# Local transformer as listed operations per engine, with the norms spread by transfers

## The chip, the cores and the metric

The kernel runs on one core of a Trainium2 chip. The metric is the device time of one execution in microseconds (us); smaller is better. A core has five engines that run their own instruction streams: TensorE (PE, matrix products, results into the PSUM memory), VectorE (DVE), ScalarE (ACT), GpSimd (POOL) and SyncE (SP, which here only issues transfers). Sixteen DMA engines move the data. Engines wait for one another through semaphores, and each works off its own instructions in the order in which they were written down.

## The reference

The program is a stack of twelve small blocks on 8 sequences of 256 tokens with 128 features. Two of its blocks are the same six-layer local transformer, and the change is in these. A layer is an attention over windows of 32 tokens that look back one window, and a gated feed-forward block. In the attention:

```python
qkv = x @ Wqkv                      # 128 -> 3 * 1024, 16 heads of 64
q = l2norm(q) * qs                  # t / max(norm(t), 1e-12)
k = l2norm(k) * ksc
q = q * cos * scale + rotate_half(q) * sin * scale
k = k * cos * inv + rotate_half(k) * sin * inv
sim = jnp.einsum('bhwie,bhwje->bhwij', bq, bk2) * QK_SCALE   # 32 rows, 64 keys
sim = jnp.where(mask, -jnp.finfo(sim.dtype).max, sim)
attn = jax.nn.softmax(sim, -1)
out = jnp.einsum('bhwij,bhwje->bhwie', attn, bv2)
return out.transpose(0, 2, 1, 3).reshape(b, n, INNER) @ Wo
```

The feed-forward block is a layer norm, a product to 2 x 341 features, `a * gelu(gate)`, and a product back to 128. Ahead of both, half of the features are shifted by one token. All numbers are 32-bit floats.

## The kernel before, in words

Activations lie features by tokens: a tile has 128 partitions (features) and T = 512 columns, two sequences of 256 tokens. There are four such groups (`NG`), and a layer treats them one after the other. A pair of layer and group is a unit. Inside a unit the sixteen heads are taken four at a time; such a *quad* is the step that the text counts in. A stage of six layers has 6 x 4 x 4 = 96 quads, and the program has two such stages.

`ffn2` is a software pipeline, written out by hand: in one pass of its loop `q0`, `q1`, `q2`, `q3` are four consecutive quads at different stages, and the calls in the loop set the order of every engine's instructions (`_Ordered` pins it). What happens to a quad:

- `quad_project` multiplies the unit's input `l_xs` by the weights of keys, then queries, into the PSUM tile `pp`. ACT squares it (`l_sq`). DVE multiplies it by the cosine table (`l_yk`, `l_yq`) and swaps neighbouring partitions (`l_yr`); POOL multiplies `l_yr` by the sine table and adds the two.
- `quad_norms` sums the squares by head on PE into `bank`; `quad_roots` turns them into inverse roots `l_rn` on ACT (a logarithm, an exponential), and SP moves four rows at a time, in four transfers, into the tile `l_rt`. In the next pass `quad_pick` spreads them over the partitions with four DVE shuffles, and `quad_keys` multiplies keys (`l_kp`) and queries (`l_yq`) by them on POOL.
- `quad_scores` forms the scores `sc`, masks included, on PE; DVE takes the maximum and subtracts it (`l_mx`, `l_e`); ACT exponentiates.
- `quad_turn` transposes the exponentials on PE (`et`) and ACT copies them (`l_at`).
- `quad_values` forms the values `vp`; ACT copies them to `l_v`, with a 65th column of ones for each head, and two SP transfers make a copy `l_w` that is shifted by one window.
- `quad_weigh` multiplies weights and values into `cx`, with the weights as the stationary operand (64x32) and the values moving (65 columns); the last column is the softmax's sum, by which DVE divides. `quad_back` transposes the result on PE (`ct`), and `quad_done` copies it (`l_ct`).

After the fourth quad, `local_rest` does the output product (`wo_acc`), the residual, the layer norm and the gated feed-forward in pieces between the quads of the next unit.

PSUM has three two-bank tiles (`two`: `pp`, `sc`, `vp`, `et`, `cx`, `ct`, `ge` take turns), one bank for sums and one for accumulators. In the profile most of these instructions carry line 285, the line of `_Ordered`'s helper, so that they are told apart by their tiles.

Of the kernel before, what the change touches and what calls it, by code (L numbers as in the profile page):

```python
# [28 lines left out]
P = 128  # L29
B, S, D = 8, 256, 128  # L30
NB = 2
# [21 lines left out]
def _constants():  # L53
# [59 lines left out]
    c["ksin"] = two(np.sin(fr) * (f(1.0) / sc) * sgn)  # L113
# [180 lines left out]
class _Net:  # L294
# [952 lines left out]
    def local_rows(self):  # L1247

        gp = self.nc.gpsimd
        one = lambda n, i, shape: self.work(f"{n}{i}", shape, bufs=1)  # L1250

        self.xs = [one("l_xs", i, (P, T)) for i in range(4)]
        for t in self.xs:
            gp.memset(t[64:, 0::S], 0.0)
        self.n_pad = 0

        self.rt = one("l_rt", 0, (P, T))
        gp.memset(self.rt, 0.0)
        self.low_masks(("lrow", "lmask"))

    def window_rows(self):

        gp = self.nc.gpsimd
        one = lambda n, i, shape: self.work(f"{n}{i}", shape, bufs=1)

        self.kp = [one("l_kp", i, (P, 2 * NB, WIN + S)) for i in range(1)]
        for t in self.kp:
            gp.memset(t[:, :, :WIN], 0.0)

        self.vs = [[one(n, i, (P, 4, 4, 65)) for n in ("l_v", "l_w")] for i in range(2)]  # L1270
        for v, w in self.vs:
            gp.memset(w, 0.0)
            for t in (v, w):
                gp.memset(t[:, :, :, 64:], 1.0)
# [12 lines left out]
    def local_tables(self, i):  # L1287

        out = {}
        for k in ("kcos", "ksin", "qcos", "qsin"):  # L1290
            t = self.work("l_" + k, (P, S), bufs=2)
            scale = self.get(f"F{i}_{k[0]}_scale" + ("_p" if k[1:] == "sin" else ""))
# [4 lines left out]
    def quad_project(self, q, n):  # L1297

        nc = self.nc
        four = lambda a: a.rearrange("p j (b s) -> p (j b) s", b=NB)  # L1300
        o = S if n == "k" else 0
        pp = self.two("pp")
        for j in range(2):
            self.mm(pp[:, j, :], q.w[:, o + P * j : o + P * (j + 1)], q.xs)
        sq = self.work("l_sq", (P, 2, T), bufs=4)
        nc.scalar.activation(sq, pp, AF.Square)
        y = self.work("l_y" + n, (P, 2, T), bufs=2)
        nc.vector.tensor_tensor(four(y), four(pp), q.tab[n + "cos"], ALU.mult)
        yr = self.work("l_yr", (P, 2, T), bufs=2)
        nc.vector.stream_shuffle(yr, pp, [i ^ 1 for i in range(32)])  # L1310
        nc.gpsimd.tensor_tensor(four(yr), four(yr), q.tab[n + "sin"], ALU.mult)
        nc.gpsimd.tensor_tensor(y, y, yr, ALU.add)
        q.y[n], q.sq[n] = y, sq

    def quad_values(self, q):
        nc = self.nc
        vp = self.two("vp").rearrange("p a b -> p (a b)")
        for m in range(4):
            self.mm(vp[:, S * m : S * (m + 1)], q.xs[:, P * m : P * (m + 1)], q.w[:, 2 * S :])
        v, w = self.vs[q.n % 2]  # L1320
        nc.scalar.copy(v.rearrange("p m h d -> p (m h) d")[:, :, :64],
                       vp.rearrange("p (n d) -> p n d", d=64))
        nc.sync.dma_start(w[32:], v[:96])
        nc.sync.dma_start(w[:32, 1::2], v[96:, 0::2])
        q.v = (w, v)

    def quad_norms(self, q):  # L1330
        sp = self.ps()
        for s, (n, j) in enumerate((("k", 0), ("q", 0), ("k", 1), ("q", 1))):
            self.mm(sp[32 * s : 32 * s + 32, :], self.get("hsum"), q.sq[n][:, j, :])
        q.sums = self.work("l_rn", bufs=1)
        self.nc.vector.tensor_scalar(q.sums, sp, 1e-24, None, ALU.max)

    def quad_roots(self, q):
        nc = self.nc
        rn = q.sums
        self.act(rn, rn, AF.Ln, scale=2.0**SH)  # L1340
        self.act(rn, rn, AF.Exp, bias=self.get("eps", 3, 1), scale=-0.5)
        for s in range(4):
            nc.sync.dma_start(self.rt[s::32], rn[32 * s : 32 * s + 32 : 8, :])

    def quad_pick(self, q):
        nc = self.nc
        q.r = {}
        for n, o in (("k", 0), ("q", 1)):
            r = q.r[n] = self.work("l_sq", (P, 2, T), bufs=4)
            for j in range(2):  # L1350
                nc.vector.stream_shuffle(r[:, j, :], self.rt, [2 * j + o] * 32)

    def quad_keys(self, q):

        nc = self.nc
        q.kp = self.kp[q.n % len(self.kp)]
        seq = lambda a: a.rearrange("p j (b s) -> p (j b) s", b=NB)
        nc.gpsimd.tensor_tensor(q.kp[:, :, WIN:], seq(q.r["k"]), seq(q.y["k"]), ALU.mult)
        nc.gpsimd.tensor_tensor(q.y["q"], q.y["q"], q.r["q"], ALU.mult)

    def quad_scores(self, q):

        nc = self.nc
        sc = self.two("sc")
# [19 lines left out]
        sl = lambda a: a.rearrange("p (n k) -> p n k", k=64)  # L1384
        bc = lambda a: a.unsqueeze(2).to_broadcast([P, 16, 64])
        sv = sl(sc.rearrange("p h n -> p (h n)"))
        mx = self.work("l_mx", (P, 16), bufs=2)
        nc.vector.tensor_reduce(mx, sv, AX.X, ALU.max)
        e = self.work("l_e", (P, 2 * T), bufs=2)
        nc.vector.tensor_tensor(sl(e), sv, bc(mx), ALU.subtract)  # L1390
        q.e = e

    def quad_exp(self, q):
        self.act(q.e, q.e, AF.Exp)

    def quad_turn(self, q):

        nc = self.nc
        tp = self.two("et").rearrange("p a b -> p (a b)")
        for n in range(8):  # L1400
            nc.tensor.transpose(tp[:, P * n : P * (n + 1)], q.e[:, P * n : P * (n + 1)],
                                self.get("ident"))
        q.at = self.work("l_at", (P, 2 * T), bufs=1)
        nc.scalar.copy(q.at, tp)

    def quad_weigh(self, q):

        nc = self.nc
        q.cx = []
        for j in range(2):  # L1410
            cp = self.two("cx")[:, :, : 4 * 65].rearrange("p x (n d) -> p x n d", d=65)
            for b in range(NB):
                for h in range(2):
                    for jj in range(4):
                        for x in range(2):
                            ks = slice(64 * x, 64 * x + 64)
                            o = P * (4 * h + 2 * j + b) + 32 * jj
                            self.mm(cp[32 * jj : 32 * jj + 32, x, 2 * b + h, :],
                                    q.at[ks, o : o + 32],
                                    q.v[jj % 2][ks, 2 * b + jj // 2, 2 * j + h, :])  # L1420
            rc = self.work("l_rc", (P, 2, 4), bufs=2)
            nc.vector.reciprocal(rc, cp[:, :, :, 64])
            cx = self.work("l_cx", (P, 2, 4, 64), bufs=4)
            nc.vector.tensor_tensor(cx, cp[:, :, :, :64],
                                    rc.unsqueeze(3).to_broadcast([P, 2, 4, 64]), ALU.mult)
            q.cx.append(cx)

    def quad_back(self, q):

        nc = self.nc  # L1430
        tp = q.tp = self.two("ct")
        for j in range(2):
            to = tp[:, j, :].rearrange("p (b c x i) -> p b x c i", b=NB, c=2, x=2)
            for b in range(NB):
                for x in range(2):
                    nc.tensor.transpose(
                        to[:, b, x], q.cx[j][:, x, 2 * b : 2 * b + 2].rearrange("p h d -> p (h d)"),
                        self.get("ident"))

    def quad_done(self, q):  # L1440
        ct = self.work("l_ct", (P, 2, T), bufs=5)
        self.nc.scalar.copy(ct, q.tp)
        q.unit.ct.append(ct)

    def local_rest(self, u):


        nc, i = self.nc, u.i
        acc = self.bank1("wo_acc")

        def project(cs):
            for c in cs:
                self.mm(acc, u.w["wo"][:, c, :], u.ct[c // 2][:, c % 2, :], start=c == 0, stop=c == 7)

        project(range(3))
        yield False
        project(range(3, 6))
        yield False
        yield False
        project(range(6, 8))  # L1460
        u.x1 = self.new_x()
        nc.vector.tensor_tensor(u.x1, acc, self.ys[u.g], ALU.add)
        if i == DEPTH - 1 and u.g == NG - 1:
            self.rest = u
            return
        xs = self.shifted(u.x1)
        yield False

        yield False
        self.settle()  # L1470
        xc, r = self.scratch("ln_c"), self.scratch("ln_r")
        m = self.bank1("mean")
        self.mm(m, self.get("mean"), xs)
        nc.vector.tensor_tensor(xc, xs, m, ALU.subtract)
        sq = self.scratch("ln_sq")
        nc.scalar.activation(sq, xc, AF.Square)
        yield True
        yield True
        v = self.bank1("var")
        self.mm(v, self.get("mean"), sq)  # L1480
# [9 lines left out]
        for f in u.early:  # L1490
            f()
# [330 lines left out]
```

## Time and profile before

| | |
|---|---|
| three runs | 5218.33, 5218.47, 5227.95 us; median 5218.47 |
| profiled execution | span 5219.8 us (from the first to the last instruction; no other time of it is listed) |
| granted TensorE clock, mean | 0.973 |
| first local stage | its first product starts at 955.6 us, its last quad's at 2611.8 |
| second local stage | 2921.4 to 4556.2 |
| PE, DVE, ACT, POOL busy | 94%, 69%, 48%, 58% of the span |
| DMA | 151.76 MB, 61390 packets |

How to read it: an engine's share is an average over the whole program; the table by stretches, shown further down, says what it is inside one stage. A group of instructions has its line, engine and operation, the tiles it writes and reads, the shape and the count, then its busy time in us and the mean ns of one, then the idle time before it and what ended that.

### The profile page before, as it was taken

What the parts mean: (1) busy time and instruction counts of PE and PEld (TensorE: products, weight loads), DVE (VectorE), ACT (ScalarE), POOL (GpSimd) and SP (SyncE); (2) the same over time, 40 slices, a digit from 0 to 9 for tenths busy, and PEclk for the clock granted to TensorE, in tenths of its full rate; (3) what the DMA queues carried; (4) which work ended last, traced back from release to release, by engine and by line L of the source; (5) the groups of instructions that cost most, each with busy time, mean ns of one, the idle gap of its engine ahead of it and who ended that gap; (6) DMA issues with size and microseconds to landing.
All of it is one profiled execution on the core that took longest, in us unless ns stands there. A gap on an engine that the chain in (4) does not pass through costs nothing.

```text
span 5219.8 us, 156276 instructions
## 1 busy us (share of the span) xinstructions
PE 4887.5 (94%) x70032; PEld 2895.3 (55%) x70032; DVE 3599.4 (69%) x6390; ACT 2483.9 (48%) x3011; POOL 3033.2 (58%) x1543
## 2 busy tenths in 40 slices
PE   9999998899999999999988899999999999989889
PEld 6755764455555555555544455555555555555456
DVE  4445446777777877787745777877787778755655
ACT  2233225555555555555544455555555555543652
POOL 0011003688888887888720588888888888701520
PEclk9999998999999999999989999999999999999999
DMA  2000000111111111111000011111111111100000
GB/s 75 1 1 1 1 1 1 40 29 49 34 49 35 43 38 45 38 42 41 26 28 5 21 36 42 37 46 37 42 41 42 41 39 41 29 36 1 1 1 9
DMA packets 61390, 151.76 MB, mean 29 GB/s; under 512 B 11185, under 2 KB 25394, under 8 KB 60466
## 3 DMA queue, kind: packets, MB, share of 16 engines
q1 hardware_dynamic: 60722, 141.77, 8.9%
q8 instruction: 551, 9.03, 0.7%
q14 instruction: 117, 0.96, 0.1%
HBM read 44.93 MB, written 1.05 MB: 9 GB/s over the span
## 4 chain that ended last, share of the span: by engine, by line
PE 71%; DVE 14%; ACT 8%; issue 2%; POOL 1%; DMA 1%; SPq 1%; DVEq 0%; ACTq 0%; POOLq 0%
PE mm L340 11%; PE pp L285 8%; PE e_o L340 7%; PE wo_acc L285 7%; PE bank L285 6%; PE sc L285 5%; PE vp L285 5%; PE ge L285 5%; PE cx L285 3%; PE ct L285 3%; DVE l_sq L285 3%; PE w_acc L285 2%; DVE l_yr L285 2%; PE ms L285 2%; ACT l_ct L285 2%
## 5 line engine op out<-in xcount | busy, mean ns | idle before, releaser
L285 PE MATMUL pp<-l_xs,wqkv 128*128 128x512 f32 x1536 | 693.4, 594 | 5.5 <-DMA wqkv<-in_f_wqkv 3.8
L285 POOL TENSOR_TENSOR l_kp<-l_sq,l_yk 128x1024 f32<-128x1024 f32 x192 | 456.6, 2378 | 357.4 <-DVE l_sq L285 354.2
L285 ACT COPY l_v<-vp 128x1024 f32<-128x1024 f32 x192 | 194.6, 1014 | 693.5 <-PE vp L285 693.5
L285 DVE STREAM_SHUFFLE l_sq<-l_rt 128x512 f32<-128x512 f32 x768 | 515.7, 747 | 0.1
L285 DVE STREAM_SHUFFLE l_yr<-pp 128x1024 f32<-128x1024 f32 x384 | 510.2, 1329 | 0.0
L285 PEld LDWEIGHTS pp<-l_xs,wqkv 128*128 128x128 f32 x1536 | 292.6, 191 | 356.6 <-issue 327.2
L340 PE MATMUL mm<-x,m 128*128 128x512 f32 x1024 | 479.4, 608 | 0.0
L285 POOL TENSOR_TENSOR l_yq<-l_yq,l_sq 128x1024 f32<-128x1024 f32 x192 | 476.1, 2479 | 0.1
L285 POOL TENSOR_TENSOR l_yr<-l_yr,l_ksin 128x1024 f32<-128x1024 f32 x192 | 456.5, 2378 | 24.9 <-DVE l_yr L285 24.9
L285 POOL TENSOR_TENSOR l_yq<-l_yq,l_yr 128x1024 f32<-128x1024 f32 x192 | 455.0, 2370 | 15.1
L285 POOL TENSOR_TENSOR l_yk<-l_yk,l_yr 128x1024 f32<-128x1024 f32 x192 | 454.2, 2366 | 15.0
L285 POOL TENSOR_TENSOR l_yr<-l_yr,l_qsin 128x1024 f32<-128x1024 f32 x192 | 455.0, 2370 | 0.0
L285 DVE TENSOR_REDUCE l_mx<-sc 128x16 f32<-128x1024 f32 x192 | 235.1, 1225 | 277.1 <-PE sc L285 277.1
L285 ACT ACTIVATE l_sq<-pp 128x1024 f32<-128x1024 f32 x384 | 384.1, 1013 | 54.5 <-PE pp L285 54.2
L340 PEld LDWEIGHTS e_o<-m,e_h 128*128 128x128 f32 x3072 | 363.1, 192 | 60.8 <-issue 60.3
L285 PE MATMUL vp<-wqkv,l_xs 128*128 128x256 f32 x1536 | 388.4, 396 | 2.6 <-issue 1.6
L285 PE MATMUL bank<-l_sq,sb_cs 128*32 128x512 f32 x1536 | 305.0, 617 | 67.0 <-ACT l_sq L285 66.5
L340 PE MATMUL e_o<-m,e_h 128*128 128x128 f32 x3072 | 363.6, 275 | 0.0
L285 PE MATMUL wo_acc<-l_ct,wo 128*128 128x512 f32 x768 | 360.9, 603 | 2.3 <-issue 2.3
L285 PE MATMUL cx<-l_w,l_at 64*32 64x65 f32 x12288 | 312.2, 226 | 51.0 <-ACT l_ct L285 41.1
L285 PE MATMUL sc<-l_kp,l_yq 64*32 64x64 f32 x24576 | 312.2, 228 | 22.6 <-issue 14.3
L285 PE MATMUL cx<-l_v,l_at 64*32 64x65 f32 x12288 | 318.8, 227 | 3.1 <-issue 3.1
(316 smaller groups left out, 9566.9 us busy)
## 6 DMA issues: line engine op xcount, KB each, us to landing
l_w<-l_v SPq DMA_DIRECT2D x192, 390.0 KB
wqkv<-in_f_wqkv SPq DMA_DIRECT2D x48, 384.0 KB
l_w<-l_v SPq DMA_DIRECT2D x192, 65.0 KB
l_rt<-l_rn SPq DMA_DIRECT2D x768, 8.0 KB
wo<-in_f_wo SPq DMA_DIRECT2D x12, 512.0 KB
m<-in_m_w SPq DMA_DIRECT2D x16, 256.0 KB
w<-in_f_w SPq DMA_DIRECT2D x12, 341.0 KB
w<-in_f_w SPq DMA_DIRECT2D x12, 192.0 KB
```

The lines of the kernel that those rows point to most:

```text
L285: r = f(*args, **kw)
L340: self.nc.tensor.matmul(out, lhsT=lhsT, rhs=rhs, start=start, stop=stop)
```

## The change

It replaces the hand-written pipeline of the two local stages by a list of small operations (`op_...`), one engine's instructions each. `ORDER` gives every engine (and "DMA" for SP's transfers) its operations in order; the number after a name says how many quads the operation lags behind. `AFTER` says what must be written down before an operation, `HELD` which PSUM places it takes and what frees them. `ffn2` writes the operations out from these lists. What is done differs in four places:

- The inverse norms go from `l_rn` to full-height tiles `l_nk` and `l_nq` by four transfers (`spread`), each of which reads four rows 32 times. The tile `l_rt` and the four shuffles go.
- Of the keys, the sine product is made on VectorE from PSUM (`kz`), then swapped (`shufk`); the sine table is permuted to match. Of the queries it stays on GpSimd.
- The exponentials are summed on VectorE (`sum`), divided on GpSimd (`ediv`) and then transposed. The column of ones goes; `l_v` and `l_w` are 64 wide.
- In `cx` the values are stationary (64x64) and the weights move (32 columns), so the result comes out turned; the `ct` transposes go, and ACT copies `cx` to `l_ct` in another order.

The diff, cut to its core:

```diff
-    c["ksin"] = two(np.sin(fr) * (f(1.0) / sc) * sgn)
+    c["ksin"] = two(np.sin(fr) * (f(1.0) / sc) * sgn)[p ^ 1]
...
-        self.rt = one("l_rt", 0, (P, T))
-        gp.memset(self.rt, 0.0)
...
+    def square(self, q, n):
+        sq = q.sq[n] = self.work("l_s" + n, (P, 2, T), bufs=1)
+        self.nc.scalar.activation(sq, q.pp[n], AF.Square)
...
+    def cosines(self, q, n):
+        y = q.y[n] = self.work("l_y" + n, (P, 2, T), bufs=2)
+        self.nc.vector.tensor_tensor(
+            self.heads(y), self.heads(q.pp[n]), q.unit.tab[n + "cos"], ALU.mult)
...
+    def sines(self, q, n):
+        z = q.z[n] = self.work("l_z" + n, (P, 2, T), bufs=1)
+        self.nc.vector.tensor_tensor(
+            self.heads(z), self.heads(q.pp[n]), q.unit.tab[n + "sin"], ALU.mult)
+
+    def partners(self, q, n, a):
+        yr = q.yr[n] = self.work("l_r" + n, (P, 2, T), bufs=1)
+        self.nc.vector.stream_shuffle(yr, a, [i ^ 1 for i in range(32)])
...
-        for s in range(4):
-            nc.sync.dma_start(self.rt[s::32], rn[32 * s : 32 * s + 32 : 8, :])
-
-    def quad_pick(self, q):
-        nc = self.nc
-        q.r = {}
-        for n, o in (("k", 0), ("q", 1)):
-            r = q.r[n] = self.work("l_sq", (P, 2, T), bufs=4)
-            for j in range(2):
-                nc.vector.stream_shuffle(r[:, j, :], self.rt, [2 * j + o] * 32)
...
+    def op_rex(self, q):
+        self.act(q.rn, q.rn, AF.Exp, bias=self.get("eps", 3, 1), scale=-0.5)
+
+    def spread(self, q, n):
+        r = q.r[n] = self.work("l_n" + n, (P, 2, T), bufs=1)
+        for j in range(2):
+            s = 32 * (2 * j + (n == "q"))
+            self.nc.sync.dma_start(
+                r[:, j, :],
+                q.rn[s : s + 32 : 8, :].unsqueeze(1).to_broadcast([4, 32, T]))
+
+    def op_kshuf(self, q):
+        self.spread(q, "k")
+
+    def op_qshuf(self, q):
+        self.spread(q, "q")
+
+    def op_kscale(self, q):
+        q.kp = self.kp[q.n % len(self.kp)]
+        self.nc.gpsimd.tensor_tensor(
+            q.kp[:, :, WIN:], self.heads(q.r["k"]), self.heads(q.y["k"]), ALU.mult)
+
+    def op_qscale(self, q):
+        self.nc.gpsimd.tensor_tensor(q.y["q"], q.y["q"], q.r["q"], ALU.mult)
...
+    def op_sum(self, q):
+        q.den = self.work("l_den", (P, 16), bufs=2)
+        self.nc.vector.tensor_reduce(q.den, self.keys64(q.e), AX.X, ALU.add)
+        self.nc.vector.reciprocal(q.den, q.den)
+
+    def op_ediv(self, q):
+        e = self.keys64(q.e)
+        self.nc.gpsimd.tensor_tensor(e, e, q.den.unsqueeze(2).to_broadcast([P, 16, 64]), ALU.mult)
...
+    def op_cx(self, q):
+        q.cx = self.two("cx")
         for j in range(2):
             for b in range(NB):
+                for jj in range(4):
+                    to = 256 * j + 128 * b + 32 * jj
+                    for h in range(2):
                         for x in range(2):
                             ks = slice(64 * x, 64 * x + 64)
                             o = P * (4 * h + 2 * j + b) + 32 * jj
-                            self.mm(cp[32 * jj : 32 * jj + 32, x, 2 * b + h, :],
-                                    q.at[ks, o : o + 32],
-                                    q.v[jj % 2][ks, 2 * b + jj // 2, 2 * j + h, :])
+                            self.mm(q.cx[64 * h : 64 * h + 64, x, to : to + 32],
+                                    q.v[jj % 2][ks, 2 * b + jj // 2, 2 * j + h, :],
+                                    q.at[ks, o : o + 32])
...
-        tp = q.tp = self.two("ct")
-        for j in range(2):
-            to = tp[:, j, :].rearrange("p (b c x i) -> p b x c i", b=NB, c=2, x=2)
-            for b in range(NB):
-                for x in range(2):
-                    nc.tensor.transpose(
-                        to[:, b, x], q.cx[j][:, x, 2 * b : 2 * b + 2].rearrange("p h d -> p (h d)"),
-                        self.get("ident"))
...
+    def op_ct(self, q):
+        ct = self.work("l_ct", (P, 2, T), bufs=5)
+        self.nc.scalar.copy(
+            ct.rearrange("p j (n x c) -> p x (j n) c", x=2, c=64),
+            q.cx.rearrange("p x (n c) -> p x n c", c=64))
...
+    ORDER = {
+        "PE": (
+            "ppk.0 ppq.0 wo2.5 cx.4 norms.0 ge0.6 ge1.6 ge2.6 wo1.4 mean.5 w20.6 w21.7 "
+            "vp.2 wo0.3 var.5 et.3 sc.1"
+        ),
+        "ACT": (
+            "rln.1 at.4 rex.1 sqk.0 aff.6 sqq.0 xsA.5 ct.4 inA.0 lsq.5 exp.2 tab1.6 "
+            "gl0.6 gl1.6 lln.5 lex.5 gl2.6 tab2.6 v.2"
+        ),
+        "DVE": (
+            "max.2 sub.2 kz.0 cosk.0 x1.5 cosq.0 shufq.0 xc.5 ag0.6 ag1.6 x2.7 nmax.0 "
+            "shufk.0 ag2.6 sum.2 hn.5"
+        ),
+        "POOL": (
+            "ediv.3 qadd.1 xsP.5 qscale.1 kscale.1 inP.0 qsin.0 kadd.0"
+        ),
+        "DMA": (
+            "kshuf.1 qshuf.1 vs.2"
+        ),
+    }
+    AFTER = {
...
+        "et": "ediv.0",
+        "sc": "kscale.0 qscale.0",
...
+        "at": "et.0 cx.1",
+        "rex": "rln.0",
...
+        "qscale": "qshuf.0 qadd.0",
+        "kscale": "kshuf.0 kadd.0 sc.1",
...
+        "kshuf": "rex.0 kscale.1",
+        "qshuf": "rex.0 qscale.1",
+        "vs": "v.0",
+    }
...
+    PLACES = {"psp2": 3, "bank": 1, "acc": 1}
```

## The prediction, made before the result was known

> **What bounds the kernel now.** I read the page first. TensorE (PE) is busy for 94% of the span at a granted clock of nine tenths or more, and the chain of work that ended last runs over PE for 71% of the span.
>
> ```profile
> span 5219.8 us, 156276 instructions
> PE 4887.5 (94%) x70032; PEld 2895.3 (55%) x70032; DVE 3599.4 (69%) x6390; ACT 2483.9 (48%) x3011; POOL 3033.2 (58%) x1543
> PE 71%; DVE 14%; ACT 8%; issue 2%; POOL 1%; DMA 1%; SPq 1%; DVEq 0%; ACTq 0%; POOLq 0%
> ```
>
> The change touches only the two local-transformer stages. I therefore took busy times by stretch in the steady part of each (columns: stretch, its length, then busy us of PE, weight loads, DVE, ACT, POOL, the clock, DMA share, GB/s), and after them the same view for the matmuls that write `ct` and `cx` alone.
>
> ```profile
> 1100.00:2600.00 1500.00, 1431.95 (x26329) 829.15 (x26328) 1182.15 (x1981) 801.08 (x930) 1243.88 (x560) 0.99 0.14 40
> 3050.00:4550.00 1500.00, 1434.11 (x26508) 831.12 (x26495) 1187.86 (x1987) 803.00 (x932) 1247.29 (x559) 0.99 0.14 40
> ...
> 1100.00:2600.00 1500.00, 96.55 (x685) 76.10 (x686) 86.09 (x85) 0.99 0.14 40
> ...
> 1100.00:2600.00 1500.00, 144.45 (x10880) 118.92 (x10880) 145.04 (x340) 0.99 0.14 40
> ```
>
> The first stretch holds 86 quads (86 instructions of each once-a-quad group), so a quad takes 1500/86 = 17.44 us, of which PE works 16.65, POOL 14.5, DVE 13.7 and ACT 9.3. PE sets the pace. `ct` is 1.12 us of PE per quad, `cx` 1.68.
>
> The third reading is the transfers. The first answer below is for the stretch 2000 to 2004, in which SP issues the four small norm transfers of one quad; the next is for 1401 to 1406, with the two window copies `l_w<-l_v` alone; the last is for 1317 to 1317.7, the thick of such a copy. "Share" is busy time over 16 DMA engines. The timeline line says when SP issued the four.
>
> ```profile
> GB/s 0 0 0 0 0 0 0 0 0 0 0 0 41 41 0 0 0 0 0 82 0 0 0 0 61 21 0 0 0 0 82 0 0 0 0 0 0 0 0 0
> DMA packets 32, 0.03 MB, mean 8 GB/s; under 512 B 16, under 2 KB 16, under 8 KB 32
> q1 hardware_dynamic: 32, 0.03, 2.4%
> ...
> DMA packets 192, 0.47 MB, mean 93 GB/s; under 512 B 32, under 2 KB 96, under 8 KB 192
> q1 hardware_dynamic: 192, 0.47, 32.3%
> ...
> DMA packets 40, 0.17 MB, mean 238 GB/s; under 512 B 0, under 2 KB 0, under 8 KB 40
> q1 hardware_dynamic: 40, 0.17, 101.0%
> ...
> 2000.10 2.27 SPq L1343 DMA_DIRECT2D l_rt<-l_rn  x4
> ```
>
> The reader is to see three things. A transfer of four rows leaves four 2 KB packets and four tiny ones (32 packets, 16 under 512 B, for four transfers), while the copies of 96 and 32 rows leave 16 tiny ones each (32 for two): one tiny packet for each DMA engine used, so four rows run on four engines. A lone 2 KB packet costs 0.024 x 16 x 4 us / 16 = 96 ns with its tiny one, about 90 without. And in a long copy engines get in each other's way: 0.323 x 16 x 5 us = 25.8 us for 0.47 MB is 114 ns for 2 KB; in the thick of it 1.01 x 16 x 0.7 / 40 = 283 ns for 4160 B, or 139 ns for 2 KB. The first packet moves 1.2 us after the issue (slices of 0.1 us).
>
> ```profile
> L285 POOL TENSOR_TENSOR l_yq<-l_yq,l_sq 128x1024 f32<-128x1024 f32 x192 | 476.1, 2479 | 0.1
> L285 POOL TENSOR_TENSOR l_yr<-l_yr,l_ksin 128x1024 f32<-128x1024 f32 x192 | 456.5, 2378 | 24.9 <-DVE l_yr L285 24.9
> L285 ACT COPY l_at<-et 128x1024 f32<-128x1024 f32 x192 | 193.7, 1009 | 111.7 <-PE et L285 111.7
> L285 ACT ACTIVATE l_rn<-l_rn,sb_c 128x512 f32<-128x512 f32 x192 | 138.7, 722 | 6.2
> ```
>
> These groups (mean ns of one after the comma) price the links of the new chain.
>
> **The change part by part**, per quad.
>
> PE: the eight `ct` transposes go, -1.12. `cx` keeps 64 calls, now with 64 weight columns instead of 32 and 32 moving columns instead of 65. Half as many moving columns bound it below at 0.84, twice the weight columns above at 3.36; the number of instructions is unchanged, so I stay near the old row and take 1.9. Idle time was 17.44 - 16.65 = 0.79; the wait for the second `cx` bank goes, and I leave 0.5. PE alone would then need 16.65 - 1.12 + 0.22 + 0.5 = 16.25 us.
>
> DVE: four `l_sq<-l_rt` shuffles go (starts 0.64 apart, 2.6), and two context products with reciprocals (2 x 0.89); the keys' sine product comes (1.21, as the cosine product), a sum and a reciprocal (1.22 as the maximum, + 0.2). About 12.0 remain under PE's 16: nothing. If that cover went, it would still be nothing, since it falls.
>
> POOL: the keys' sine product leaves, the division comes. Its row is the product it replaces, 2.38, also with a broadcast operand; if its broadcast were free it costs no less, if it doubled POOL had 16.6. Six operations, 14.2 us, hidden in either case under the chain below.
>
> ACT: the same eight passes; the `ct` copy reads in another order, hidden (9.3 of 17.4). SP: six issues as before, 0.57 each (2.27/4); weights that wait behind them have slack of a layer. POOL's other waits: `xsP` waits for `x1`, with `qscale`, `kscale` behind it, but these wait longer for the norms anyway.
>
> The norms: `spread` replaces 8 KB transfers of four rows by four of 256 KB, each reading four rows 32 times into 128 partitions: 128 packets of 2 KB. The source still counts four rows outermost, so I take four engines, 32 packets each, by the row above. Whether four transfers in a row take the same four engines no row shows; shape and queue are the same each time and I take the same, so one engine moves 128 packets a quad. If each took its own four, the last would land after 1.2 + 3 x 0.57 + 32 x 0.114 = 6.6 us.
>
> The page "DMA: Bandwidth & Descriptors" of the Trainium skill (section "Why a DMA increments its semaphore by 16 and not by 1", on how many engines) speaks against the change: the count is the largest number up to 16 that divides the outermost size on both sides, and the lowest-numbered engines are used. By it 4 and 128 give four, the same four each time; the rows agree with the count (four tiny packets) and are silent on which, so by the page the sum below stands and the 6.6 us fall away.
>
> Price of a packet: 90 ns alone, 139 in the thick. Sustained bursts of several engines into SBUF are nearest to the whole copy: 114. Then the last of the four lands 1.2 + 128 x 0.114 + 0.1 = 15.9 us after the first issue.
>
> What is late next is the loop over quads. `l_nk` and `l_nq` have one buffer, so `kshuf` of a quad waits for `kscale` of the quad before, and `qshuf` stands behind it on SP. On POOL `qscale` comes before `kscale` and needs the transfer that lands last. So from one `kscale` to the next: 15.9 + 2.48 + 2.38 = 20.7 us (rounded down, since POOL's starts are a little closer than its durations). `sc` waits for `kscale` on PE, and everything of the next quad stands behind it. The other way round the loop, from `et` over `at` (1.01) and `rex` (0.72), asks for PE's work plus 1.8. In the heaviest quad, with three `ge` chunks (121.8 us for 22 units in the first stretch, 5.5) and a third of `w2` (66.2/22/3 = 1.0), against 4.4 of such work on average, that is 15.75 + 2.1 - 0.3 for overlaps + 1.8 = 19.3, and does not bind. Two stages have 2 x 95 steps: 190 x (20.7 - 17.44) = +619. The tail of each stage grows by a sum and a division (1.4 + 2.4): +8. Sum +627 against the span of 5219.8, which lies 1.3 us above the median of the three runs (its own time is not listed apart): 5845 beside the median.
>
> Both ends: at 90 ns the landing takes 12.8, the loop 17.65, and the gelu quad adds 1.6 in four: 18.05, so +124 and 5343. At 139 ns it takes 19.1 and 23.9: +1235 and 6454.
>
> The page "SBUF — State Buffer" (section on the DMA port swizzle) puts partitions 0 to 31 and 32 to 63 on the same ports of 27.2 GB/s; two of the four engines would then write one port in step, an estimate of 150 ns a packet, a loop of 25.4 and some 6740 us. No row here separates ports.
>
> **The rivals.** First, not slower: the spread lands early because it runs on more engines, or on four different ones each time (6.6 us). Then PE's 16.25 sets the pace: 190 x (16.25 - 17.44) + 8 = -218, 5000 us. For it: DMA is idle to 86% (share 0.14). Against it: the four tiny packets. It decides when the landing takes less than 12.6 us, where the loop falls under 17.44.
>
> Second, PE stays the bound but `cx` doubles through its weight columns (3.36): 16.25 + 1.46 = 17.7, +50 + 8, about 5276. For it: weight loads are already 118.92 of `cx`'s 144.45; against it: they overlap there. It needs the early landing too.
>
> Third, POOL becomes the bound through a division of twice the price: 16.6 us a quad, still faster than now, 5068; it too needs the early landing.
>
> **How the numbers follow.** Loop 0.82; early landing with PE as the bound 0.12, with POOL 0.01; with doubled `cx` 0.05. A measurement of this kernel tells 0.2% (10 us) from nothing. The range runs from the doubled `cx` with a little room, 5250, to the dear packets, 6460; it leaves out the early landing (0.13) and a packet dearer than 139 ns (some 0.07). The likeliest case's own range is 5343 to 6454. Faster: the early landing and a hundredth of the loop, 0.14. The doubled `cx` is split, 0.03 same and 0.02 slower; slower is 0.81 + 0.02 = 0.83.
>
> **What would show it.** Right: PE's busy share falls far under 94%; the longest waits are POOL's `l_yq` or `l_kp` for a DMA `l_nq`; four `spread` transfers take over 12 us from issue to the last byte, DMA share near 0.3 with 512 spread packets a quad; `ct` matmuls are gone. Wrong: PE still at 95% in the stages and POOL waiting for DVE; then four engines, or the same four, was the false step. A quad of over 24 us would mean dearer packets.

## The result and the profile after

The changed kernel takes 5633.4 us (5622.1 to 5643.9), the kernel before, on the same chip, 5220.9 us (5218.3 to 5228.0): a ratio of 1.0787, with a 95% interval of 1.0768 to 1.0805. The forecast was 5845 us, with a range of 5250 to 6460. So the sign and the range held, and the forecast was 212 us too high, which is half of the loss of 412 us. How that half comes about takes up most of what follows, because two errors of opposite sign are in it.

The page of the changed kernel first: the span, the busy times, and the engines' shares of the chain that ended last.

```profile
span 5620.1 us, 151536 instructions
...
PE 4846.3 (86%) x68496; PEld 2901.2 (52%) x68496; DVE 3299.6 (59%) x4662; ACT 2474.2 (44%) x3011; POOL 2914.4 (52%) x1531
...
PE 42%; DMA 26%; POOL 13%; ACT 6%; SPq 6%; DVE 4%; issue 3%; POOLq 0%; ACTq 0%; DVEq 0%
```

PE fell from 94% to 86% busy and from 71% to 42% of the chain; transfers rose from 1% to 26%. The next view is the busy time by stretch in the two local stages (PE, weight loads, DVE, ACT, POOL, granted clock, DMA share, GB/s), and then the same for `cx` alone.

```profile
1100.00:2600.00 1500.00, 1285.41 (x23505) 758.08 (x23506) 960.01 (x1106) 728.73 (x854) 1094.64 (x513) 0.93 0.27 89
3050.00:4550.00 1500.00, 1286.95 (x22959) 753.40 (x22958) 969.46 (x1126) 729.35 (x847) 1040.25 (x492) 0.94 0.25 84
...
1100.00:2600.00 1500.00, 161.79 (x9984) 153.02 (x9984) 78.94 (x78) 0.93 0.27 89
```

The first stretch now holds 78 quads (the copies out of `cx`) instead of 86; its first 135 us still belong to the long quads at the stage's start. `cx` takes 161.79/78 = 2.07 us a quad. The clock went from 0.99 to 0.93 and 0.94 and the DMA share from 0.14 to 0.27 and 0.25. What the engines wait for is in the list of waits (us in total, times, longest).

```profile
POOL l_yq L285 <- DMA l_nq<-l_rn: 1018.9, 191, 13.8
...
PE sc L285 <- POOL l_kp L285: 557.9, 172, 14.3
...
DVE l_mx L285 <- PE sc L285: 443.4, 171, 8.9
```

This is the wait that the prediction named: GpSimd stands before `qscale` for the last spread transfer, 5.3 us a quad on average, and PE stands before `sc` behind it. The transfers themselves are seen best in the thick of one spread. This is the DMA view of the stretch 1506 to 1512 (busy tenths of the 16 engines in 40 slices, packets, and the queue's share).

```profile
DMA  2222222212222222122222222222222222222282
...
DMA packets 304, 0.61 MB, mean 102 GB/s; under 512 B 12, under 2 KB 12, under 8 KB 303
...
q1 hardware_dynamic: 303, 0.60, 26.0%
```

The share lies at a quarter almost without a break: four of sixteen engines work and twelve stand idle. The price of a packet is 0.26 x 16 x 6 us / 303 = 82 ns. Over the packet records from 1400 to 2400 the median of 2 KB is 84 ns and the mean 88.

Last, the chain of work around one quad in the steady part (start, us, what), with short pieces left out.

```profile
1500.41 0.90 ACT l_at L285
1501.31 0.63 ACT l_rn L285
...
1502.00 0.58 SPq L1401
...
1504.46 10.61 DMA l_nq<-l_rn
...
1515.27 2.33 POOL l_yq L285
1517.60 2.31 POOL l_kp L285
1519.91 0.02 issue
1519.92 0.58 SPq L1401
```

From the first issue (1502.00) to the start of `qscale` (1515.27) it takes 13.3 us. Then `qscale` and `kscale` run, and 0.02 us after `kscale` the next quad's first transfer is issued. That is the loop over the one buffer, as the prediction wrote it down; from issue to issue it is 17.92 us here.

Where the 400.3 us of span went, from the starts of each quad's first product:

| | before | after | difference |
|---|---|---|---|
| quads 20 to 84 of stage 1, mean | 17.37 us | 18.56 us | |
| quads 20 to 84 of stage 2, mean | 17.31 us | 18.36 us | |
| all 95 steps of stage 1, mean | 17.43 us | 19.59 us | +205 us |
| all 95 steps of stage 2, mean | 17.21 us | 18.58 us | +130 us |
| stage 1's last quad to stage 2's first | 309.6 us | 348.9 us | +39 us |
| last quad to the end | 663.5 us | 694.4 us | +31 us |

The start of stage 1 is 5 us earlier. In steady quads the loss is some 1.1 us. Taking those means for all quads, against the mean of all steps before, 95 x (18.56 - 17.43) + 95 x (18.36 - 17.21) = 217 us. Another 119 us are longer quads at the stages' edges: 19 of the changed kernel's quads last over 23 us, 15 of them in stage 1, all among the first twelve or the last four steps of a stage.

### The profile page after: what moved, and what is told of

It reads as the page before. It is cut to its first block, busy times and chain, and to the rows that moved or that the text cites. A ratio compares the mean times of both kernels' runs of the same rounds, so it can differ in the third digit from the quotient of the medians.

```text
span 5620.1 us, 151536 instructions
## 1 busy us (share of the span) xinstructions
PE 4846.3 (86%) x68496; PEld 2901.2 (52%) x68496; DVE 3299.6 (59%) x4662; ACT 2474.2 (44%) x3011; POOL 2914.4 (52%) x1531
## 3 DMA queue, kind: packets, MB, share of 16 engines
q1 hardware_dynamic: 155954, 335.43, 17.6%
q8 instruction: 538, 8.81, 0.6%
## 4 chain that ended last, share of the span: by engine, by line
PE 42%; DMA 26%; POOL 13%; ACT 6%; SPq 6%; DVE 4%; issue 3%; POOLq 0%; ACTq 0%; DVEq 0%
DMA l_nq<-l_rn 26%; PE mm L340 10%; PE e_o L340 6%; PE pp L285 6%; SPq L1401 6%; POOL l_yq L285 5%; POOL l_kp L285 5%; PE bank L285 4%; PE sc L285 2%; PE cx L285 2%; PE ge L285 2%; PE ms L285 2%; ACT l_rn L285 1%; PE wo_acc L285 1%; PE av L285 1%
## 5 line engine op out<-in xcount | busy, mean ns | idle before, releaser
L285 POOL TENSOR_TENSOR l_yq<-l_yq,l_nq 128x1024 f32<-128x1024 f32 x192 | 454.0, 2365 | 1020.8 <-DMA l_nq<-l_rn 1018.9
L285 PEld LDWEIGHTS sc<-l_kp,l_yq 64*32 64x32 f32 x24576 | 304.2, 120 | 614.3 <-POOL l_kp L285 609.5
L285 POOL TENSOR_TENSOR l_rq<-l_rq,l_qsin 128x1024 f32<-128x1024 f32 x192 | 471.7, 2457 | 17.7 <-DVE l_rq L285 17.7
L285 POOL TENSOR_TENSOR l_yq<-l_yq,l_rq 128x1024 f32<-128x1024 f32 x192 | 457.1, 2381 | 0.0
L285 POOL TENSOR_TENSOR l_yk<-l_yk,l_rk 128x1024 f32<-128x1024 f32 x192 | 453.0, 2359 | 0.0
L285 POOL TENSOR_TENSOR l_kp<-l_nk,l_yk 128x1024 f32<-128x1024 f32 x192 | 452.5, 2357 | 0.0
L285 PEld LDWEIGHTS cx<-l_at,l_w 64*64 64x64 f32 x12288 | 332.9, 136 | 166.9 <-issue 140.2
L285 PE MATMUL cx<-l_at,l_w 64*64 64x32 f32 x12288 | 380.9, 222 | 20.8 <-ACT l_at L285 11.7
L285 POOL TENSOR_TENSOR l_e<-l_e,l_den 128x1024 f32<-128x1024 f32 x192 | 365.4, 1903 | 32.7 <-ACT l_v L285 32.7
L285 PE MATMUL cx<-l_at,l_v 64*64 64x32 f32 x12288 | 378.4, 220 | 3.4 <-issue 3.4
```

What stands on the lines that cost most here:

```text
L285: r = f(*args, **kw)
```

## The experiments

**Sixteen engines and two engines instead of four.** By `hsum` the first sixteen rows of each group of 32 in `l_rn` are alike, and so are the last sixteen. So the source can count more rows with fewer copies, or fewer rows with more copies, and write the same numbers.

```diff
-                q.rn[s : s + 32 : 8, :].unsqueeze(1).to_broadcast([4, 32, T]))
+                q.rn[s : s + 32, :].unsqueeze(1).to_broadcast([32, 4, T]))
```

> The spread's source now counts 32 rows outermost, four copies of each, instead of four rows, 32 copies of each; the data written are the same. Theory (four DMA engines make the landing late, and the late landing sets the pace): the transfers leave sixteen tiny packets each, an engine carries 32 packets of 2 KB a quad instead of 128, the last of the four lands about 1.2 + 3 x 0.57 + 32 x 0.086 = 5.7 us after the first issue, the loop from kscale to kscale is 10.4 us, and PE sets the pace with 16.3 to 16.6 us a quad: 4990 to 5130 us. Rival (the other parts cost it: cx with twice the weight columns, the new order of the lists, the pieces of neighbouring stages): the quad stays at 18 us and the time above 5250.

For two engines the line reads `q.rn[s : s + 32 : 16, :]...to_broadcast([2, 64, T])`.

> The source counts two rows outermost, 64 copies of each. Theory: two engines, 256 packets each a quad; 256 x 0.086 = 22.0 us, landing 23.3 us after the issue, loop 23.3 + 4.65 = 28.0 us a quad: 190 x (28.0 - 18.3) = +1840, some 7400 us (7200 to 7700). Rival (four engines hinder one another, or the transfers share one limit of bytes a second): two engines work faster each, and the time stays under 6700.

Two engines: 7512.8 us (one run), inside the theory's 7200 to 7700. This is the DMA view of its stretch 1715 to 1725,

```profile
DMA  1111111111111111111111131111111111111111
...
q1 hardware_dynamic: 246, 0.50, 13.0%
```

and the longest wait in its list:

```profile
POOL l_yq L285 <- DMA l_nq<-l_rn: 2904.8, 192, 23.2
```

The share is 13%, two engines of sixteen; a packet costs 0.13 x 16 x 10 us / 246 = 85 ns, the same as with four; and the quads of the steady part last 27.8 to 29.1 us (mean 28.3 in both stages), where 28.0 had been worked out. So the engines do not hinder one another, the same two take every transfer, and the loop over the one buffer has the right terms.

Sixteen engines: 5215.9 us, a ratio of 1.0003 (0.9976 to 1.0031): the loss is gone, but not a microsecond beyond it. The theory had said 4990 to 5130. Most quads did become short (13.8 to 17.3 us), but in the two stages together 22 lasted 25 to 28 us. The timeline of one such quad shows why (start, us, engine, instruction, and in brackets the idle time before it).

```profile
1654.48 0.63 ACT L285 ACTIVATE l_lr<-l_lr 128x512 f32<-128x512 f32 x1
1654.59 2.36 POOL L285 TENSOR_TENSOR l_rq<-l_rq,l_qsin 128x1024 f32<-128x1024 f32 x1
...
1655.15 8.81 DVE L285 TENSOR_TENSOR l_hn<-l_lc,l_lr 128x512 f32<-128x512 f32 x1
...
1656.26 3.70 PE L285 MATMUL pp<-l_xs,wqkv 128*128 128x512 f32 x8
...
1656.92 2.34 POOL L285 TENSOR_TENSOR l_yk<-l_yk,l_rk 128x1024 f32<-128x1024 f32 x1
...
1659.22 1.89 POOL L285 TENSOR_TENSOR l_e<-l_e,l_den 128x1024 f32<-128x1024 f32 x1
...
1661.08 2.33 POOL L285 TENSOR_TENSOR l_yq<-l_yq,l_rq 128x1024 f32<-128x1024 f32 x1
1663.88 1.21 DVE L285 TENSOR_REDUCE l_mx<-sc 128x16 f32<-128x1024 f32 x1
...
1666.46 0.44 PE L285 MATMUL cx<-l_at,l_w 64*64 64x32 f32 x8 [6.49 <-issue]
```

The layer norm's product `hn` takes 0.69 us where nothing holds it up. Here it "takes" 8.81, as it does (over 8 us) in 20 of its 46 executions: it starts as soon as its root is there (1654.48 + 0.63), while GpSimd is busy, and it ends 0.55 us after the fourth of four GpSimd products that follow one another without a gap (1661.08 + 2.33 = 1663.41). VectorE stands still meanwhile, and PE waits 6.49 us before `cx`. VectorE's other large instructions beside the same GpSimd products keep their length: those with one operand in PSUM (1.21) or with one operand at all.

**The spread alone undone.** Transfers of four rows into `l_rt` and four shuffles on VectorE again, the rest as in the changed kernel.

```diff
+    def pick(self, q, n):
+        r = q.r[n] = self.work("l_n" + n, (P, 2, T), bufs=1)
+        for j in range(2):
+            self.nc.vector.stream_shuffle(r[:, j, :], self.rt, [2 * j + (n == "q")] * 32)
...
+            self.nc.sync.dma_start(self.rt[s::32], q.rn[32 * s : 32 * s + 32 : 8, :])
...
-            "max.2 sub.2 kz.0 cosk.0 x1.5 cosq.0 shufq.0 xc.5 ag0.6 ag1.6 x2.7 nmax.0 "
+            "max.2 sub.2 kz.0 cosk.0 qpick.1 kpick.1 x1.5 cosq.0 shufq.0 xc.5 ag0.6 ag1.6 x2.7 nmax.0 "
...
```

> The spread alone is undone: four transfers of four rows into l_rt and four VectorE shuffles, as before the change; the operation lists, the keys' sine product, the division ahead of the turning and the turned cx stay. Theory (the spread costs all, the other parts save the ct transposes): PE sets the pace with 16.3 to 16.6 us a quad, DVE has 12.0 + 2.6 = 14.6 under it: 5000 to 5100 us. Rival (the other parts cost too: cx at 3.36 us, or the lists' order): 5200 us or more.

5415.7 us, a ratio of 1.0379 (1.0361 to 1.0396): slower than before, without any spread. So the theory fell: the spread is not the only cost. Three quads in four last 13.8 to 16.5 us; the fourth lasts 25 to 27.5, because there `hn` is long in nearly every unit (over 8 us in 43 of 46). The answer for that tile (ns, min/median/max):

```profile
L285 DVE TENSOR_TENSOR l_hn<-l_lc,l_lr x46: 691/8470/8491, 1098.5 to 4759.6; 128x512 f32<-128x512 f32 x46
```

In the changed kernel itself the same instruction has a median of 1980 ns and a maximum of 2909: GpSimd waits 5 us a quad for the landing there, and `hn` gets its turn.

**`hn` with one operand in PSUM.** The root is written into the PSUM bank of the variance instead of SBUF; the arithmetic is the same.

```diff
-        self.act(u.r, u.r, AF.Exp, scale=-0.5)
+        self.act(u.v, u.r, AF.Exp, scale=-0.5)
...
-        self.nc.vector.tensor_tensor(u.hn, u.xc, u.r, ALU.mult)
+        self.nc.vector.tensor_tensor(u.hn, u.xc, u.v, ALU.mult)
...
-        "var": ("acc", "lln"),
+        "var": ("acc", "hn"),
```

With sixteen engines:

> As the run with sixteen engines, and the inverse root of the layer norm (lex) is written to PSUM instead of SBUF, so that the VectorE product hn = l_lc x root has one operand in SBUF instead of two. Theory (hn with two SBUF operands cannot start beside GpSimd's products, and with the spread early GpSimd runs four to six of them without a gap, so hn takes 8.8 us, and the PSUM places that VectorE should free come late): hn takes 0.7 us every time, the 21 quads of about 26.5 us become 17.2, 21 x 9.3 = 195 us less: 5020 us (4970 to 5070). Rival (hn waits for its own input or for the logarithm, not for GpSimd): the long quads stay and the time is 5180 or more.

5038.2 us, ratio 0.9641 (0.9610 to 0.9672), inside the theory's range. With the shuffles:

> As the run with the spread undone, and the same edit of hn. There every fourth quad lasts 25.9 instead of 16.4 us, 46 times hn took 8.5 us. Theory: 46 x 9.4 = 430 us less: 4985 us (4930 to 5050). Rival: 5380 or more.

5082.6 us, ratio 0.9733 (0.9718 to 0.9747): 333 us less than without the edit. The theory's range ended at 5050; its mechanism holds, its gain of 430 us was too large, since this fourth quad still takes 17.6 to 18.6 us and not 16.4. In the version with sixteen engines the answer for `hn` now reads

```profile
L285 DVE TENSOR_TENSOR l_hn<-l_lc,var x46: 686/689/692, 1103.5 to 4384.7; 128x512 f32<-128x512 f32 x46
```

and the stretch 1400 to 2400 of its stage 1 (same columns as above):

```profile
1400.00:2400.00 1000.00, 976.41 (x18882) 579.45 (x18875) 742.61 (x882) 578.93 (x676) 867.27 (x410) 0.99 0.42 108
```

All 46 take 0.69 us. PE is busy for 97.6% at a clock of 0.99, with 15.95 us for a steady quad of stage 1: here PE is the bound again. And with the changed kernel's four engines:

> The changed kernel (four engines, one buffer) with the same edit of hn alone. Theory: there GpSimd waits 5 us a quad for the landing, hn finds it idle soon and takes 1.8 us; it stands beside the landing, so no more than 46 x 1.1 = 50 us can go and likely none does: 5585 to 5640 us. Rival (the same stall is the main cost of the change): under 5500 us.

5652.6 us (one run): 13 us above the theory's range, and nothing gained. The same wait costs 333 us behind the shuffles, some 180 us behind the early landing, and nothing behind the late one.

The page "SBUF — State Buffer" of the Trainium skill (section "Who interferes with whom") says that a VectorE instruction with two operands in SBUF needs a read interface that it shares with GpSimd, which one of them then holds for a whole instruction. The runs agree in the main: `hn` with two SBUF operands is hit, and with one it is not. Two operands are not the only form that was stretched, though: in the run with sixteen engines the small table products `l_kcos<-sb_cs,sb_pv` (0.35 us at least) reached 1.99 us, for a cause that was not looked into. The runs show one thing more: at the three seams between the four GpSimd products VectorE did not get its turn, so that the wait lasts for the whole run of products and not for one.

**Two buffers.** Four engines as in the changed kernel, but two buffers each for `l_nk`, `l_nq` and `l_rn`.

```diff
-        r = q.r[n] = self.work("l_n" + n, (P, 2, T), bufs=1)
+        r = q.r[n] = self.work("l_n" + n, (P, 2, T), bufs=2)
...
-        "kshuf": "rex.0 kscale.1",
-        "qshuf": "rex.0 qscale.1",
+        "kshuf": "rex.0 kscale.2",
+        "qshuf": "rex.0 qscale.2",
```

> Four engines as in the changed kernel, but l_nk, l_nq and l_rn have two buffers each, so that a quad's transfers need not wait for the products of the quad before. Theory 1 (the loop over the one buffer is what limits): an engine's 128 packets take 11 us a quad, less than PE's 16.3, so the time falls to 5000 to 5150. Theory 2 (the chain et, at, rex, landing, qscale, kscale, sc, which closes over two quads, limits nearly as much): from et's start 0.9 + 1.0 + 0.63 + 13.2 + 4.65 = 20.4 to sc, and from sc's start 15.3 of PE's work to the next et, (20.4 + 15.3) / 2 = 17.9 us a quad; the time falls only to 5450 to 5600.

5694.9 us, ratio 1.0906 (1.0887 to 1.0925). Theory 1 is refuted: the loop over the one buffer is gone, and nothing is gained. Theory 2 is nearer, though it too had expected less. The chain of work of this run, over two quads:

```profile
1717.85 0.63 ACT l_rn L285
1718.49 0.91 ACT l_at L285
1719.39 0.63 ACT l_rn L285
...
1722.58 11.11 DMA l_nq<-l_rn
...
1736.15 2.35 POOL l_kp L285
...
1738.55 2.05 PE sc L285 x128
1740.60 5.22 PE pp L285 x8
1745.82 2.00 PE cx L285 x128
...
1753.31 0.89 PE et L285 x8
1754.26 0.64 ACT l_rn L285
1754.89 0.90 ACT l_at L285
1755.79 0.63 ACT l_rn L285
```

From `rex` to `rex` (1719.39 to 1755.79) 36.4 us pass, through one landing and then nearly all of PE's work for a quad, and two quads lie in them: 18.2 us a quad, of which no buffer takes anything away. The mean was 18.93 us in the steady part; the 0.7 us between the two are not accounted for. Theory 2 had 17.9, with 15.3 us for PE's share from `sc` to the next `et`; here that took 14.8. What the theory left out is the logarithm `rln` (0.64) ahead of `at`, and from `rex` to `sc` it took 19.2 us instead of 18.5. On ACT `rln` stands behind the copy of the values,

```profile
1753.35 1.01 ACT L285 COPY l_v<-vp 128x1024 f32<-128x1024 f32 x1 [2.73 <-PE vp L285]
```

which ends 0.16 us after `et`, so that the way into the roots leads from `vp` through this copy as much as through `et`. Why the run is slower than the changed kernel by 61 us is not settled.

If this chain is the bound, then moving the copy `at` (0.9 us) off it must show, at half its length a quad:

```diff
-            "rln.1 at.4 rex.1 sqk.0 aff.6 sqq.0 xsA.5 ct.4 inA.0 lsq.5 exp.2 tab1.6 "
+            "rln.1 rex.1 at.4 sqk.0 aff.6 sqq.0 xsA.5 ct.4 inA.0 lsq.5 exp.2 tab1.6 "
```

> The run with four engines and two buffers, and on ACT the exponential of the root (rex) stands ahead of the copy at instead of behind it. Theory (with two buffers the bound is the chain et, at, rex, four issues, landing, qscale, kscale, sc, next et, which closes over two quads): at (0.9 us), and what waits for et, leave the chain that is walked once in two quads, so a quad gets 0.45 to 0.9 us shorter: 190 x 0.45 to 0.9 = 85 to 170 us less than 5695: 5525 to 5610 us. Rival (the engines' throughput or SP's issues limit): 5680 or more.

5608.4 us, ratio 1.0735 (1.0717 to 1.0753): 86 us less, 0.45 us a quad. This is at the edge of the theory's range. It speaks for the chain and against the rival, and the gain is no more than that of `at` alone; the steady quads of the profiled executions fell by 0.35 us, from 18.93 to 18.58.

With the early landing, two buffers should do nothing:

> Sixteen engines, hn from PSUM, and two buffers for l_nk, l_nq and l_rn. Theory (with an early landing the loop over the one buffer, 10.4 us, does not bind, since PE needs 15.3 a quad): the same as without the second buffers, within 0.5%. Rival (the 18-us quads at the start of each stage, some 14 in all, run at the pace of that loop with GpSimd's six products in it): 14 x 2.7 = 40 us less.

5046.5 us, ratio 0.9666 (0.9650 to 0.9682), against 0.9641 (0.9610 to 0.9672) without them: no difference that these runs can tell. The rival's 40 us are not there.

**The long quads at the edges.** In the changed kernel, pieces of the neighbouring stages are written down between the quads. The chain around 1080 shows what that does:

```profile
1075.67 2.32 POOL l_yq L285
1078.00 2.31 POOL l_kp L285
...
1080.35 2.06 PE sc L285 x121
1082.41 2.02 PE bank L285 x2
...
1084.45 0.70 DVE ln_c L285
...
1085.70 0.61 ACT l_rn L285
1086.32 0.90 ACT l_at L285
1087.22 0.63 ACT l_rn L285
...
1090.39 11.19 DMA l_nq<-l_rn
```

The loop is longer here: after `kscale` come `sc`, then a product of another stage's norm (`bank`, `ln_c`), and only then the roots, the copy and the next landing. That is about 26 us a quad. The edit takes those pieces out of the loop (they are written down together where a unit asks for its input, or after the stage):

```diff
-            if self.set == LN_EXP:
-                self.pump()
             t += 1
```

> The changed kernel without the pieces of the neighbouring stages between the quads: they are written down all together where a unit first asks for its input, or after the stage. The work is the same. Theory (the quads of 24 to 26 us at the beginning and end of the stages, some 20 of them, come from those pieces: bank products behind sc on PE, ln_c, ln_sq and the root ahead of rln, at and rex, on the way to the late landing): these quads fall to 18.3 us, 20 x 6.5 = 130 us less; three bursts at the start of each stage and the pieces after it give some 50 to 80 back: 5633 - 65 = 5570 us (5530 to 5610). Rival (the long quads come from the start of the pipeline itself, or the pieces cost as much in bursts): 5625 us or more.

5553.7 us, ratio 1.0641 (1.0625 to 1.0657), within the theory's 5530 to 5610: 80 us less. Of the quads of 23 to 26 us at the start of stage 1 the first still takes 23, eight became 17 to 20.5, and two bursts of 38 and 39 us stand in place of the others.

**What beats both kernels.** Sixteen engines, `hn` from PSUM and no pieces between the quads, and the same with `rex` ahead of `at`:

> Sixteen engines, hn from PSUM, and no pieces between the quads. Theory: with the early landing the pieces cost less there (quads of 18 instead of 15.5 us at the start: some 14 x 2.5 = 35 us), and bursts give as much back: 5038 us within 0.6% (5010 to 5070). Rival (pieces between quads are what holds it above its 15.9 us a quad): 4990 us or less.

> The same edit on the version with sixteen engines, hn from PSUM and no pieces between the quads. Theory (there PE is the bound, 15.9 us a quad with 0.4 idle): at comes later by 0.63 us and the landing earlier; no gain beyond 0.3%, 4995 to 5030 us. Rival (the landing is still on the path in the quads of 17 us): 4960 us or less.

5011.7 us, ratio 0.9605 (0.9589 to 0.9621), and 4997.8 us, ratio 0.9569 (0.9551 to 0.9587). Both lie where the theories had put them, near the lower ends. In the last version, with these repairs, the change is worth 4.3% instead of costing 7.9%. The kernel before has a layer-norm product with two SBUF operands too (`t<-ln_c,ln_r`, 1.88 us at the median in its local stages); what reading one from PSUM would gain there was not tried, so not all of the 4.3% need belong to the change.

## Why the prediction was right, and where it was wrong

**Four engines, the same four each time.** Right. The share is a quarter, two engines give an eighth, and the time follows: 28.3 us a quad with two engines where the sum says 28.0. As the Trainium skill's page "DMA: Bandwidth & Descriptors" has it (section "Why a DMA increments its semaphore by 16 and not by 1"), the outermost sizes of source and destination decide. With a source of 32 rows and the same data it takes 7.6 us (median) from the first issue to `qscale`, with four rows 12.8; for 32 rows 5.7 to the landing had been worked out.

**The price of a packet.** Wrong, and it is the term that carried the forecast too high. I took 114 ns, because bursts of several engines seemed nearest to the long copy of before. It was 88 ns on the mean (median 84), the lone packet's price. A long burst does not make packets dear. They were dear only in the run with sixteen engines, with a mean of 134 ns, though half of them took 84 there too; with two engines the mean was 89. That it is the number of engines which does it, and not what ran beside them, is not shown. With 88 ns the landing is 1.2 + 128 x 0.088 + 0.1 = 12.6 us (12.8 measured at the median from the issue to `qscale`) instead of 15.9, and the loop 17.4 instead of 20.7. The shortest steps measured from `kscale` to `kscale` were 17.4, which is no more than the old quad: with the right price the forecast's own loop would have cost next to nothing. The prediction's own low end for this case, worked out at 90 ns, was 5343, which is 290 us under the 5633 measured. So it is in part luck that the middle came within 212 us: what the sum left out made up for nearly half of what its packet price put in. The estimate by port sharing, 150 ns a packet, has nothing for it in these runs. The sign "a quad of over 24 us would mean dearer packets" misled as well: 16 quads last longer than that, and from 962 to 1236 us, where ten of them lie, packets took 91 ns on the mean.

**Which loop binds.** Half right. The loop over the one buffer is there, and with two engines it rules alone. But at 88 ns a packet it is shorter than another, of which the prediction said "does not bind" in its middle case (at 90 ns it let this path add 1.6 us in one quad of four): from `et` over `at` and `rex` through a landing, the two products and `sc`, and through PE's order to the next `et`. That sum had counted PE's work plus 1.8 us and left the landing out, as if it were always the buffer's. It closes over two quads and takes 18.2 to 18.9 us a quad where two buffers leave it alone; taking away the one buffer therefore brought nothing. With one buffer both are at work: of the 128 steps from `kscale` to `kscale` in the steady parts of the changed kernel 60 last 17.4 to 17.6 us, the loop over the buffer to the tenth, 28 up to 18.6, and 40 longer. What came last before the first issue of a quad says which of the two it was: 63 times `kscale`, with steps of 17.46 us at the median, and 65 times `rex`, on the mean 1.6 us after `kscale`, with steps of 18.90. Of the 134 us by which the 128 steps exceed 17.42, 126 lie behind `rex`. With two buffers half of the steps fall to 13.5 to 16 us, and the other half grow to 20 to 25, so that the mean is no better. So the loop term of 619 us was 217 us in truth, and the late landing costs nearly all of them by a chain that the prediction had ruled out in its middle case.

**What was left out.** The pieces of the neighbouring stages, which stand on the way to the landing at the stages' edges (119 us of longer quads; 80 us came back when the pieces were moved), and the ends of the stages: +39 and +31 us where +8 stood. These ends are long in every variant (329 to 374 us and 669 to 715 us against 309.6 and 663.5), and with the spread undone they still are (333 and 690), so most of it belongs to other parts of the change than the spread. Which of them does it was not tried. Against the profiled execution (5620.1) the forecast is 225 us too high: 619 - 217 = 402 us too much in the loop term, less the 119 us of edges, less 39 + 31 - 8 = 62 us of ends, plus the 5 us by which the first stage starts earlier, which makes 226.

**PE, POOL and DVE.** `cx` at 2.07 us (taken: 1.9) and PE's own need were about right: with the early landing and `hn` mended, a quad takes 15.9 us on the mean of the steady parts, with 0.37 idle, where 16.25 and 0.5 were said. The division takes 1.90 us instead of 2.38, and stays hidden. For DVE the prediction said that its cover could go without a price, because its work falls. In the changed kernel it did cost nothing. But VectorE's time is not its work alone: with the cover gone, one instruction's wait for GpSimd costs 180 to 330 us.

**The rivals.** "Early landing, PE sets the pace, 5000 us" is what the chip does once the landing is early and `hn` is out of GpSimd's way (5038, at best 4998); the early landing by itself gave 5216. That third bound was in no rival. Neither the doubled `cx` nor a doubled division occurred.

## What to carry to other kernels

A transfer's speed inside the chip can hang on how its source is counted: look at the number of tiny packets in the old transfers, and give a broadcast as many outer rows as there are engines. When a landing is late, write down every chain that passes through it, also those that close over two steps of the pipeline, before a second buffer is spent on one of them. After a stall is removed, look next for a VectorE product with two SBUF operands beside long runs of GpSimd products: it can cost ten times its length, and reading one operand from PSUM takes it out of the way.

## What the hardware showed that was not expected

- A VectorE product of 0.69 us waited up to 8.8 us, through four GpSimd products that followed one another, and was recorded as busy all the while. "Busy" VectorE time in such a stretch is not work: 224 us for 46 instructions in the run with sixteen engines, 32 us with one operand in PSUM (46 x 0.69).
- Packets of 2 KB within SBUF took 84 ns at the median whether two, four or sixteen engines worked; the mean was 89 with two, 88 with four and 134 with sixteen, where a quarter of the packets took over 145. Four engines together cost nothing: a lone packet of the kernel before took 88.
- The granted clock goes with PE's idle time. In the steady parts (quads 20 to 84) it is 0.99 where PE idles 0.37 us a quad (sixteen engines, `hn` mended), 0.94 and 0.95 where it idles 2.3 (the changed kernel), and 0.78 where it idles 11 (two engines). Its records hold only full and half clock, 134 stretches of each in the changed kernel, and the 128x512 product of `pp` shows both: 592 or 593 ns at the median in all three runs, while those of over 1 us (none, 140 and 303 in the steady parts, at most 1.22 us) all start 1.6 to 4.8 us after the end of a wait of PE of over 1 us. By these its mean over the run rises from 612 to 682 and 758 (594 before), so a wait is paid a second time in the products behind it. Which products pay depends on where the wait stands: with the spread undone PE idles 2.0 us a quad at a clock of 0.94 and 0.95, yet `pp` stays at 612 on the mean, and `cx`, which stands behind the wait for `hn`, takes 2.49 us a quad instead of the 2.09 with `hn` from PSUM.
